# A two-layer graph network on one core: norms applied in halves, and layer 1's unit ends moved behind a copy

## The chip, the core and the metric

The kernel runs on one core of one Trainium2 chip. Its engines work side by side, each through its own list in order, and wait for one another by semaphores: TensorE (PE; its weight loads are PEld), VectorE (DVE), ScalarE (ACT), GpSimd (POOL), and SyncE (SP), which issues most of the transfers. The metric is device time of one launch in microseconds. The kernel before takes 3890.02 us, the median of 3 runs (3889.3 to 3892.25).

## The reference, cut to what matters

Eight graphs of 2048 nodes with 256 features share one adjacency matrix. Layer 0 is masked attention with a softmax inside each chunk of 256 keys, added over the chunks; layer 1 is graph attention. Each is followed by norms over the features:

```
# layer 0: four heads of 64, keys in chunks of 256
scores = clip(q . k / 8, -10, 10);  scores = where(mask == 0, -10, scores)
ctx = sum over chunks of softmax(scores within the chunk) @ v
out = layernorm(ctx @ Wo.T + bo + x) * gamma + beta
x   = layernorm(x + out)
# layer 1: four heads of 64
e = leaky_relu(s_src[j] + s_dst[i], 0.2), masked;  alpha = softmax(e)
x = layernorm(x + elu(alpha @ (x @ W)))
```

## The kernel before, in words

The order of the work is written out by hand (line 89). One program serves the eight graphs ("batches"). While batch b is in layer 0, batch b-1 is in layer 1 and batch b-2 in its closing norm, all interleaved.

Layer 0 of a batch is 64 *slots*. A slot is one chunk of 256 keys against 512 queries for two heads; 16 slots make a group of 512 queries, and the four groups are called q 0 to 3; i is the slot's place in the group. In slot s TensorE runs, in this order: scores of slot s+1 (`ps`, L360); the product of the first head (`pc`, L393); three tiles of layer 1 (`pa`, L709); the product of the second head (`pc` again). The two products share one PSUM buffer, since their pool has a single one (line 83), and ScalarE's copy to `raw` (L400) empties it each time. VectorE clips and masks the scores (`pr`, L371), inverts the sums (`rd`, L408), and makes layer 1's `e` (L689), one step of three tiles ahead of their use. ScalarE takes exponentials of `pr` (L383).

Layer 1 has 12 *units* of 16 tiles in a batch. At three tiles per slot a unit ends in slots i = 5, 10 and 15 of each group. Its end is a generator, `close` (L726), of four steps: `dn` (L732, 733) on VectorE; `hh` (L737), five or six activations on ScalarE; `ee` and `hp` (L741, 743) on ScalarE; `h` (L745) on VectorE. `rest(1)` runs one step. It is called at the head of `step` (L754), so between the two products of a slot: after the exponentials and ahead of the second head's copy.

`Between` carries the finished group of 512 queries from layer 0 to layer 1. Its steps are hung on slots by three tables: `AHEAD` at a slot's start, `BESIDE` after the scores (VectorE's share), `BEHIND` after the second copy. Two norms apply there: the first (`a.apply`, slot 7), then `scale` by gamma, `again` (the residual), statistics, the second (`finish`, slot 11). `Norm.apply` (L471) is four activations, one for each block of 128 nodes. `finish` also stores the result to DRAM (`x1D`, L533, from ScalarE's queue). `load` (slot 12) reads it back on SyncE's queue in squares of 32 (`x1t`, eight transfers, L262), `turn` (slot 14) transposes it on VectorE (`x1T`, L274), and `values` multiplies it by layer 1's weights (`pw`, L552) from slot 14 on. The last group of a batch goes another way, between the batches.

`Closing` does the same for the last norm: `add`, `stats` and `finish` (applied to `o`) in slots of q 0, as `CLOSING` says.

The tables of before:

```
AHEAD  = {12: load}
BESIDE = {..., 8: scale, 9: again + b2.stats((0, 1)), 10: b2.stats((2, 3)), 14: turn}
BEHIND = {..., 7: a.apply(y), 11: finish, 14: values((0,)), 15: values((1,))}
```

Of the kernel before, what the change touches and what calls it, by code (L numbers as in the profile page):

```python
# [8 lines left out]
F32 = mybir.dt.float32  # L9
# [8 lines left out]
P = 128  # L18
# [4 lines left out]
def adj_resnorm_kernel(  # L23
# [19 lines left out]
    nc = tc.nc  # L43
    B, N, F = x.shape
# [11 lines left out]
    QT = CH // P  # L56
# [23 lines left out]
    blocks = ctx.enter_context(tc.tile_pool(name="blocks", bufs=2))  # L80
# [28 lines left out]
    x1D = tc.dram_tile([B, N, F], F32, name="x1D")  # L109
# [75 lines left out]
    outgoing = []  # L185
# [61 lines left out]
    def by_node(dram, b, g):  # L247

        return dram[b, g * CH : (g + 1) * CH, :].rearrange("(t p) f -> p t f", p=P)
# [94 lines left out]
    def load_slab(s):  # L344
        q, hp, c = where[s]
        slab = slabs.tile([P, KT, CH], I8, tag="slab", name="slab")
        nc.sync.dma_start(out=slab, in_=clipD[q][:, KT * c : KT * (c + 1), :])
        slab_of[s] = slab
# [98 lines left out]
    class Norm:  # L447
# [20 lines left out]
                nc.gpsimd.tensor_tensor(self.rs, self.rs, nhalf, ALU.pow)  # L468
                nc.gpsimd.tensor_mul(self.off, self.off, self.rs)

        def apply(self, dst):  # L471
            for k in range(QT):
                nc.scalar.activation(  # L473
                    dst[:, k, :],
                    self.src[:, k, :],
                    AF.Identity,
                    bias=self.off[:, k : k + 1],
                    scale=self.rs[:, k : k + 1],
                )


    class Between:
# [45 lines left out]
            nc.vector.tensor_add(self.y, self.y, self.r)  # L528
            self.b2 = Norm(self.y, "b")

        def finish(self):
            self.b2.apply(self.y)
            nc.scalar.dma_start(out=by_node(x1D, self.b, self.g), in_=self.y)  # L533

        def load(self):
            self.t = load_turned(x1D, self.b, self.g, "x1t")
# [30 lines left out]

    AHEAD = {12: lambda o: o.load()}  # L570
    BESIDE = {
        1: [lambda o: o.bias()],
        4: [lambda o: o.add((0, 1))],
        5: [lambda o: o.add((2, 3)), lambda o: o.a.stats((0, 1))],
        6: [lambda o: o.a.stats((2, 3)), lambda o: o.shift()],
        8: [lambda o: o.scale()],
        9: [lambda o: o.again(), lambda o: o.b2.stats((0, 1))],
        10: [lambda o: o.b2.stats((2, 3))],
        14: [lambda o: o.turn()],
    }  # L580
    BEHIND = {
        3: lambda o: o.output((0, 1)),
        4: lambda o: o.output((2, 3)),
        7: lambda o: o.a.apply(o.y),
        11: lambda o: o.finish(),
        14: lambda o: o.values((0,)),
        15: lambda o: o.values((1,)),
    }
# [56 lines left out]
    class Layer1:  # L645
# [106 lines left out]
            )  # L752

        def step(self):  # L754
            self.rest(1)
            for _ in range(STEP):
                self.make()
                self.use()

    class Close:  # L760
# [9 lines left out]
            nc.vector.tensor_add(self.h, self.h, self.x)  # L770
            self.n = Norm(self.h, "c")

        def finish(self):
            o = blocks.tile([P, QT, F], F32, tag="y", name="o")
            self.n.apply(o)
            outgoing.append(lambda: nc.sync.dma_start(out=by_node(out, self.b, self.g), in_=o))

    class Closing:

# [4 lines left out]
        def do(self, s, beside=True, behind=True):  # L784
            for g, step in self.table.get(s, ()):
                if step == "load" and behind:
                    self.of[g] = Close(self.b, g)
                elif step == "finish" and behind:
                    self.of[g].finish()
                elif step == "add" and beside:  # L790
                    self.of[g].add()
                elif step == "stats" and beside:
                    self.of[g].n.stats((0, 1, 2, 3))
# [8 lines left out]
    for g in range(NCH):  # L802
# [11 lines left out]
        -1: [(0, "load")],  # L814
        0: [(0, "add"), (1, "load")],
        1: [(0, "stats")],
        2: [(0, "finish")],
        3: [(1, "add"), (2, "load")],
        4: [(1, "stats")],
        5: [(1, "finish")],  # L820
        7: [(2, "add"), (3, "load")],
        8: [(2, "stats")],
        10: [(2, "finish")],
        11: [(3, "add")],
        12: [(3, "stats")],
        13: [(3, "finish")],
    }
    CLOSING_ALONE = {
        -1: [(0, "load"), (1, "load")],
# [23 lines left out]
    lower = None  # L853
    for b in range(B):
        waug = blocks.tile([P, NT, H, D1], F32, tag="waug", name="waug")
        sd = small.tile([P, 2 * H, NT], F32, tag="sd", name="sd", bufs=1)
        if b == 0:
            for s in range(3):
                load_slab(s)
        scores(0)  # L860
        for u in range(KT):
            exps(0, u)
        if lower:
            for _ in range(STEP):
                lower.make()
        closing = Closing(b - 2, CLOSING) if b > 1 else None
        if closing:
            closing.do(-1)
        group = None
        for s in range(SLOTS):  # L870
            q, hp, c = where[s]
            i = s % QS
            send()
            if s + 3 < SLOTS:
                load_slab(s + 3)
            if i == 0:
                before = group
                group = Between(b, q - 1, sd, waug) if q else None
            if i == 1 and q:
                load_context(b, q - 1, 1)  # L880
            if i == QS // 2 + 1:
                load_context(b, q, 0)
            if group and i in AHEAD:
                AHEAD[i](group)
            if s == SLOTS - 1 and b + 1 < B:
                turns = [project(b + 1, g) for g in range(NCH)]
                turns[0].pop(0)()
            if s:
                normalize(s - 1)
            if s + 1 < SLOTS:  # L890
                scores(s + 1)

            if i == 3 and q:
                turn_context(q - 1, 1)
            if i == QS // 2 + 3:
                turn_context(q, 0)
            if group:
                for step in BESIDE.get(i, ()):
                    step(group)
            elif closing:  # L900
                closing.do(s, behind=False)
            product(s, 0)
            if s + 1 < SLOTS:
                for u in range(KT):
                    exps(s + 1, u)
            if lower:
                if b + 1 < B or s < SLOTS - LATE:
                    lower.step()
            elif masks.left():
                masks.step()  # L910
            product(s, 1)

            if before and i in AFTER:
                AFTER[i](before)
            if i == 0 and q:
                send_context(b, q - 1, 1)
            if i == QS // 2:
                send_context(b, q, 0)
            if group and i in BEHIND:
                BEHIND[i](group)  # L920
            elif closing and not q:
                closing.do(s, beside=False)
        normalize(SLOTS - 1)
        if lower and b + 1 < B:
            lower.rest(4)

        send()
        before = group
        gd, fs = factors(b, sd, waug)
        group = None  # L930
        every = tuple(range(QT))

        def begin():
            nonlocal group
            group = Between(b, NCH - 1, sd, waug)

        def ctx():
            context(NCH - 1, 1)

        steps = [  # L940
            lambda: group.bias(),
            lambda: group.output(every),
            lambda: group.add(every),
            lambda: (group.shift(), group.a.stats(every)),
            lambda: group.a.apply(group.y),
            lambda: (group.scale(), group.again(), group.b2.stats(every)),
            lambda: group.finish(),
            lambda: group.turn_all(),
            lambda: group.values((0, 1)),
            lambda: group.values((2, 3)),  # L950
        ]
        if b + 1 < B:
            (t0, k0, v0, q0), (l1, t1, k1, v1, q1), (l2, t2, k2, v2, q2), (l3, t3, k3, v3, q3) = turns
            order = [begin, t0, lambda: before.values((2, 3)), steps[0], k0, ctx, l1, v0, steps[1]]
            order += [t1, steps[2], q0, *steps[3:5], k1, l2, steps[5], v1, steps[6], t2, q1, l3]
            order += [steps[7], k2, steps[8], steps[9], v2, fs[0], t3, q2, fs[1], k3]
            order += [lambda: [load_slab(s) for s in range(3)], fs[2], v3, q3]
        else:

            step = lower.step  # L960
            order = [begin, lambda: before.values((2, 3)), steps[0], step, ctx, step, steps[1], step]
            order += [steps[2], step, steps[3], step, steps[4], step, steps[5], step, steps[6], step]
            order += [steps[7], step, steps[8], step, steps[9], step, fs[0], step, fs[1], step, fs[2]]
            order += [step, lambda: lower.rest(4)]
            assert sum(p is step for p in order) == LATE
        for piece in order:
            send()
            piece()
        send()
        lower = Layer1(b, gd, waug)  # L970
# [5 lines left out]
    for s in range(SLOTS + 1):  # L976
        send()
        if s < SLOTS:
            lower.step()
        else:  # L980
            lower.rest(4)
        closing.do(s)
        ending.do(s)
# [43 lines left out]
```

## Time and profile before

Time from the start of a slot's first `pc` matmul to the next slot's, batch 3, cut from the trace by hand (us). The other batches from 2 to 6 agree within 0.04 but for one slot; batch 1 has 6.03 in all of q 0, for it has no closing norm.

| i | 0 | 1 | 2 | 3 | 4 | 5 | 6 | 7 | 8 | 9 | 10 | 11 | 12 | 13 | 14 | 15 |
|---|---|---|---|---|---|---|---|---|---|---|---|---|---|---|---|---|
| q 0 | 6.03 | 6.04 | 6.60 | 6.03 | 6.03 | 6.71 | 6.03 | 6.03 | 6.03 | 6.07 | 6.03 | 6.03 | 7.13 | 6.58 | 6.03 | 6.03 |
| q 1 | 6.03 | 6.03 | 6.03 | 7.96 | 7.96 | 5.80 | 5.68 | 6.21 | 5.68 | 5.68 | 5.96 | 5.87 | 6.61 | 5.68 | 6.77 | 6.77 |
| q 2 | 6.77 | 6.77 | 5.68 | 7.61 | 7.61 | 5.68 | 5.68 | 6.12 | 5.68 | 5.68 | 5.89 | 5.87 | 6.60 | 5.68 | 6.77 | 6.77 |
| q 3 | 6.77 | 6.77 | 5.68 | 7.61 | 7.61 | 5.68 | 5.68 | 6.12 | 5.68 | 5.68 | 5.89 | 5.87 | 6.61 | 5.68 | 4.85 | |

How to read it: slots of equal content last equally long, so a longer one shows either more work for TensorE or a wait. Slots 3 and 4 hold the output projection, slots 14, 15, 0 and 1 the value projection of layer 1, up to q 1's slot 5 the units are six blocks wide, after it five. Slot 14 of q 3 has no scores behind it. Batch 0, without a layer below, has slots of 4.68 us, and so has batch 7 in the last 14 slots, whose steps of layer 1 are kept for later.

The 512 slots are about four fifths of the span of 3888.7 us; the rest are projections between the batches (67.6 us each after batches 2 to 6, from the last slot's start to the next batch's first), the start (84.0) and layer 1 of the last batch alone (267.9).

### The profile page before, as it was taken

To read this page: it belongs to the slowest core of one execution; us is meant where nothing else is said; L and a number is where in the kernel's file an instruction comes from. 1 tells how busy PE (TensorE), PEld (TensorE's weight loads), DVE (VectorE), ACT (ScalarE), POOL (GpSimd) and SP (SyncE) were. 2 spreads that over 40 slices of the span, in tenths; PEclk is the share of its full clock that TensorE was granted. 3 is DMA by queue.
4 is the path that set the end of the run, shared out by engine and by line. 5 is a ranking of instruction groups with operands and counts; after the bars stand their busy time and mean duration, and the time that the engine had idled before them with its cause. 6 is when DMAs were issued, how large, how long until landed. Compare 5 with 4: busy or idle time off the path is not lost. (4 is left out here: it accounts for less than half of the span.)

```text
span 3888.7 us, 160154 instructions
## 1 busy us (share of the span) xinstructions
PE 3696.5 (95%) x72068; PEld 2752.5 (71%) x72068; DVE 3204.7 (82%) x4810; ACT 1946.2 (50%) x3601; POOL 1384.4 (36%) x1202
## 2 busy tenths in 40 slices
PE   7988999999999999999999999999999999999787
PEld 4655577776777767776777767777677776776676
DVE  4776499985999779996999959998599977998798
ACT  3655445554555445554555545555455555555321
POOL 0444234342433333432433324434243333434310
PEclk9999999999999999999999999999999999999999
DMA  7642333333434343333433334333343334333354
GB/s 151 150 108 59 77 96 98 97 89 94 121 97 102 75 121 101 99 102 70 134 99 100 97 87 129 101 95 88 94 121 102 98 78 118 106 95 88 95 146 123
DMA packets 771328, 398.48 MB, mean 102 GB/s; under 512 B 442576, under 2 KB 735824, under 8 KB 770640
## 3 DMA queue, kind: packets, MB, share of 16 engines
q1 hardware_dynamic: 720640, 354.54, 35.9%
q10 hardware_dynamic: 50000, 33.70, 2.7%
q8 instruction: 563, 9.22, 1.0%
q14 instruction: 125, 1.02, 0.1%
HBM read 331.22 MB, written 56.89 MB: 100 GB/s over the span
## 5 line engine op out<-in xcount | busy, mean ns | idle before, releaser
L371 DVE SCALAR_TENSOR_TENSOR pr<-ps,slab 128x1024 f32<-128x1024 f32 x1024 | 1192.7, 1205 | 237.3 <-PE ps L360 234.0
L393 PEld LDWEIGHTS pc<-vaug,pr 128*64 128x64 f32 x32768 | 1041.6, 138 | 475.3 <-ACT raw L400 243.9
L689 DVE SCALAR_TENSOR_TENSOR e<-srow,gd,et 128x640 f32<-128x640 f32 (+1 forms) x1536 | 1348.0, 934 | 5.4 <-PE pa L709 5.4
L393 PE MATMUL pc<-vaug,pr 128*64 128x65 f32 x32768 | 1161.4, 224 | 68.9 <-ACT raw L400 63.1
L383 ACT ACTIVATE pr<-pr 128x1024 f32<-128x1024 f32 x1024 | 1052.1, 1057 | 249.3 <-DVE pr L371 234.5
L709 PE MATMUL pa<-waug,e 128*64 128x65 f32 x32768 | 1089.8, 224 | 41.0 <-DVE e L689 39.2
L709 PEld LDWEIGHTS pa<-waug,e 128*64 128x64 f32 x32768 | 1025.2, 139 | 70.3 <-DVE e L689 39.8
L360 PE MATMUL ps<-qT,kT 64*128 64x512 f32 x4096 | 1022.4, 617 | 9.1 <-DVE pr L371 7.0
L415 POOL TENSOR_TENSOR part<-raw,rd 128x512 f32<-128x512 f32 x448 | 467.9, 1044 | 1472.7 <-DVE rd L408 1460.1
L400 ACT COPY raw<-pc 128x260 f32<-128x260 f32 x1024 | 383.5, 375 | 1139.0 <-PE pc L393 1092.4
L417 POOL TENSOR_TENSOR acc<-acc,part 128x512 f32<-128x512 f32 x448 | 574.0, 1281 | 35.2
L360 PEld LDWEIGHTS ps<-qT,kT 64*128 64x128 f32 x4096 | 351.5, 186 | 332.1 <-issue 208.7
L408 DVE RECIPROCAL rd<-raw 128x8 f32<-128x8 f32 x512 | 101.5, 198 | 139.4 <-ACT raw L400 133.2
L415 POOL TENSOR_TENSOR acc<-raw,rd 128x512 f32<-128x512 f32 x64 | 66.8, 1043 | 366.1 <-DVE rd L408 365.3
L304 PE MATMUL pp<-xT,wk_sb 128*128 128x512 f32 x256 | 123.9, 628 | 47.0 <-DVE xT L274 32.3
L737 ACT ACTIVATE hh<-pa,dn 128x64 f32<-128x64 f32 x512 | 114.0, 319 | 101.3 <-DVE dn L733 101.3
L552 PE MATMUL pw<-w_sb,x1T 128*128 128x264 f32 x512 | 137.0, 403 | 2.6 <-DVE x1T L274 2.5
L468 POOL TENSOR_TENSOR rs_c<-rs_c,nhalf 128x4 f32<-128x4 f32 x32 | 55.6, 1738 | 227.5 <-DVE off_c L467 227.5
L508 PE MATMUL po<-wo_sb,qT 128*128 128x256 f32 x512 | 124.8, 389 | 0.0
L304 PEld LDWEIGHTS pp<-xT,wk_sb 128*128 128x128 f32 x256 | 48.3, 198 | 106.5 <-issue 49.6
L320 PE MATMUL pv<-wv_sb,xT 128*128 128x256 f32 x512 | 115.9, 379 | 0.0
L304 PE MATMUL pp<-xT,wq_sb 128*128 128x512 f32 x256 | 115.3, 593 | 0.0
(90 smaller groups left out, 1888.2 us busy)
## 6 DMA issues: line engine op xcount, KB each, us to landing
et<-edgeD SPq DMA_DIRECT2D x256, 320.0 KB, 3.2
slab<-clipD SPq DMA_DIRECT2D x512, 128.0 KB, 3.5
et<-edgeD SPq DMA_DIRECT2D x128, 384.0 KB, 3.5
srow<-rowD SPq DMA_DIRECT2D x64, 320.0 KB, 4.4
xp<-in_x_dram SPq DMA_DIRECT2D x256, 64.0 KB, 2.3
xg<-in_x_dram SPq DMA_DIRECT2D x32, 512.0 KB, 4.7
x1D<-y ACTq DMA_DIRECT2D x32, 512.0 KB, 3.1
x1g<-x1D SPq DMA_DIRECT2D x32, 512.0 KB, 5.9
```

Source lines behind the costliest of these rows:

```text
L304: nc.tensor.matmul(pp[:, c, :], lhsT=w[:, kc, c * P : (c + 1) * P], rhs=st["xT"][:, kc, :], start=(kc == 0), stop=(kc == KC - 1),)
L360: nc.tensor.matmul(ps[:, k, :], lhsT=kT[rows, hp, t * P : (t + 1) * P], rhs=qT[rows, hp, cols], start=True, stop=True,)
L371: nc.vector.scalar_tensor_tensor(pr, pss[u], -CLIP, slab[:, u, :].unsqueeze(1).to_broadcast([P, 2, CH]), op0=ALU.max, op1=ALU.min,)
L383: nc.scalar.activation(pr, pr, AF.Exp, scale=0.125)
L393: nc.tensor.matmul(pc[z * D : (z + 1) * D, i, :], lhsT=probs[s][u][:, k, i * P + z * D : i * P + (z + 1) * D], rhs=vaug[:, KT * c + u, 2 * ...
L400: nc.scalar.copy(raws[s][:, k], pc)
L415: nc.gpsimd.tensor_mul(part, raw[:, :, :, :D], rd.to_broadcast([P, 2, QT, D]))
L417: nc.gpsimd.tensor_add(accv, accv, part)
L508: nc.tensor.matmul(po[:, k, :], lhsT=qT[:, c, t * P : (t + 1) * P], rhs=wo_sb[:, c, :], start=(c == 0), stop=(c == KC - 1),)
L552: nc.tensor.matmul(pw[:, k, : F + 2 * H], lhsT=self.x1T[:, c, u * P : (u + 1) * P], rhs=w1_sb[:, c, :], start=(c == 0), stop=(c == KC - 1),)
L689: nc.vector.scalar_tensor_tensor(e[:, :w], self.rows[n][:, :w], self.gd[:, h, j : j + 1], self.edge[k // JG][:, j % JG, :w], op0=ALU.max, ...
L709: nc.tensor.matmul(self.pa[z * D : (z + 1) * D, i * D1 : (i + 1) * D1], lhsT=e[:, i * P + z * D : i * P + (z + 1) * D], rhs=self.waug[:, j ...
```

## The change

Each application of a norm is split into two blocks and two blocks, in neighbouring slots, so that no slot has all four on ScalarE. What depends on it moves along: `scale` from slot 8 to 9, the end of `finish` with its store from 11 to 12, `load` from 12 to 13; `turn` and `values` stay. And `rest(1)`, the step at a unit's end, goes from the head of `step` to behind the second product, so that ScalarE copies the second head's sums ahead of it. It is meant to keep ScalarE's long runs out of the way of the copies for which TensorE waits.

```diff
-        def apply(self, dst):
-            for k in range(QT):
+        def apply(self, dst, ks=range(QT)):
+            for k in ks:
...
-        def finish(self):
-            self.b2.apply(self.y)
-            nc.scalar.dma_start(out=by_node(x1D, self.b, self.g), in_=self.y)
+        def finish(self, ks=range(QT)):
+            self.b2.apply(self.y, ks)
+            if ks[-1] == QT - 1:
+                nc.scalar.dma_start(out=by_node(x1D, self.b, self.g), in_=self.y)
...
-    AHEAD = {12: lambda o: o.load()}
+    AHEAD = {13: lambda o: o.load()}
...
-        8: [lambda o: o.scale()],
-        9: [lambda o: o.again(), lambda o: o.b2.stats((0, 1))],
+        9: [lambda o: o.scale(), lambda o: o.again(), lambda o: o.b2.stats((0, 1))],
...
-        7: lambda o: o.a.apply(o.y),
-        11: lambda o: o.finish(),
+        7: lambda o: o.a.apply(o.y, (0, 1)),
+        8: lambda o: o.a.apply(o.y, (2, 3)),
+        11: lambda o: o.finish((0, 1)),
+        12: lambda o: o.finish((2, 3)),
...
         def step(self):
-            self.rest(1)
             for _ in range(STEP):
...
-        2: [(0, "finish")],
-        3: [(1, "add"), (2, "load")],
+        2: [(0, "half")],
+        3: [(0, "rest"), (1, "add"), (2, "load")],
         4: [(1, "stats")],
-        5: [(1, "finish")],
+        5: [(1, "half")],
+        6: [(1, "rest")],
...
-        10: [(2, "finish")],
+        9: [(2, "half")],
+        10: [(2, "rest")],
...
-        13: [(3, "finish")],
+        13: [(3, "half")],
+        14: [(3, "rest")],
...
             product(s, 1)
+            if lower:
+                lower.rest(1)
```

Outside the slots (between the batches and in the last batch's layer 1 alone) `rest(1)` is called ahead of `step` as before, and norms are applied whole.

More of the change, by code (lines that the diff above doesn't have):

```diff
@@ L771, in add, with finish @@
             self.n = Norm(self.h, "c")
[L773 to L776, printed above, removed]
+        def finish(self, ks=range(QT)):
+            if ks[0] == 0:
+                self.o = blocks.tile([P, QT, F], F32, tag="y", name="o")
+            self.n.apply(self.o, ks)
+            if ks[-1] == QT - 1:
+                outgoing.append(
+                    lambda: nc.sync.dma_start(out=by_node(out, self.b, self.g), in_=self.o)
+                )
     class Closing:
@@ L787, in do @@
                     self.of[g] = Close(self.b, g)
+                elif step == "half" and behind:
+                    self.of[g].finish((0, 1))
+                elif step == "rest" and behind:
+                    self.of[g].finish((2, 3))
                 elif step == "finish" and behind:
@@ L958, in adj_resnorm_kernel, with step @@
         else:
-            step = lower.step
+            def step():
+                lower.rest(1)
+                lower.step()
             order = [begin, lambda: before.values((2, 3)), steps[0], step, ctx, step, steps[1], step]
@@ L978, in adj_resnorm_kernel @@
         if s < SLOTS:
+            lower.rest(1)
             lower.step()
```

## The prediction

> **What bounds the kernel now.** I read four views in order: engine totals, wait list, the trace cut at the slots, and the timeline of one disputed stretch. The totals:
>
> ```profile
> PE 3696.5 (95%) x72068; PEld 2752.5 (71%) x72068; DVE 3204.7 (82%) x4810; ACT 1946.2 (50%) x3601; POOL 1384.4 (36%) x1202
> ```
>
> TensorE is nearly full and ScalarE half empty, so shortening ScalarE's work alone buys nothing; only a wait that reaches TensorE counts. The wait list (total us, times, longest) says which do:
>
> ```profile
> PEld pc L393 <- ACT raw L400: 243.9, 284, 3.1
> ...
> PE pc L393 <- ACT raw L400: 63.1, 104, 2.3
> ...
> PE pa L709 <- DVE e L689: 39.2, 33, 5.5
> ```
>
> The second line, 63.1 us, is the true idle time in which a product waits for the copy that empties its only PSUM buffer; the first includes waits of weight loads behind running matmuls. 63 us is the pool the change can draw on.
>
> Cutting the trace at the first `pc` matmul of each slot (table above) shows where: slots without a wait last 5.68 us (6.03 with six-bank units, 6.77 with a value projection). Over that floor lie, in q 1 to 3, slot 7 (+0.44 to +0.53), 10 (+0.21), 11 (+0.19) and 12 (+0.92); in q 0, slots 2 and 5 (+0.6, +0.7), 12 (+1.10) and 13 (+0.55). The timeline of q 2's slots 12 to 14 (start, duration):
>
> ```profile
> 1672.98 2.08 ACT L473 ACTIVATE y<-y,off_b,rs_b 128x256 f32<-128x256 f32 x4
> ...
> 1675.09 0.37 ACTq L533 DMA_DIRECT2D x1D<-y  x1
> ...
> 1676.21 2.19 ACT L383 ACTIVATE pr<-pr 128x1024 f32<-128x1024 f32 x2 [0.28 <-DVE pr L371]
> ...
> 1678.01 5.62 SPq L262 DMA_DIRECT2D x1t<-x1D  x8
> 1678.30 1.11 ACT L737 ACTIVATE hh<-pa,dn 128x64 f32<-128x64 f32 x5
> 1679.28 0.40 ACT L400 COPY raw<-pc 128x260 f32<-128x260 f32 x1
> 1679.73 1.15 PE L393 MATMUL pc<-vaug,pr 128*64 128x65 f32 x32 [0.68 <-ACT raw L400]
> ...
> 1683.24 0.45 ACT L741 ACTIVATE ee<-hh 128x320 f32<-128x320 f32 x1
> ...
> 1687.11 1.23 DVE L274 STREAM_TRANSPOSE x1T<-x1t 128x1024 f32<-128x1024 f32 x1
> ```
>
> See two things. `hh` stands before the copy, and `pc` waits for it: that is what the change removes. And `x1D` leaves at 1675.09, its re-read `x1t` begins only 2.92 us later, takes 5.62 us to issue, and `x1T` needs it at 1687.11: that is the chain the change moves.
>
> [...] SyncE waits for this store all 24 times:
>
> ```profile
> SPq L262 <- DMA x1D<-y: 199.7, 24, 12.0
> ```
>
> [...] VectorE idled for `x1t` in one of 24 turns. [...] `raw` (1679.28) starts only as `hh` (1678.30 + 1.11) ends.
>
> **The change, part by part.** No computation is added; instructions change places.
>
> *Unit's end behind the copy.* `dn` moves from slots 6, 11, 0 to the end of 5, 10, 15, `hh` to the end of 6, 11, 0, `ee`/`hp` to 7, 12, 1, `h` to 8, 13, 2. In q 1 to 3, slot 12: exps end at 1678.4, the copy is then done by 1678.7, so only the scores hold slot 13. `dn` and its reciprocal (0.12 and 0.19, start to start 0.26) now stand ahead of slot 11's `pr`, which shifts slot 12's start from 1673.13 to about 1673.3; from there `pc`, `pa`, `pc` and the scores reach slot 13 at 1679.17 instead of 1679.73. I take this 0.56 as the net saving, hence T14 (slot 14's start) 1684.85 in place of 1685.41.
>
> Slot 7: the same mechanism, but I cost it at nothing, since VectorE is full there:
>
> ```profile
> 1650.00:1679.00 29.00, 28.92 (x660) 22.16 (x660) 28.89 (x46) 18.40 (x33) 12.68 (x11) 1.00 0.35 91
> ```
>
> The columns are stretch, length, busy time of PE, PEld, DVE, ACT, POOL; VectorE works 28.89 of 29.00 us. TensorE starting slot 8 at 1649.5 in place of 1650.0 meets the same queue: in after's order `rd, pr, e, h, rd, pr, scale, again, stats, e, rd, pr`, with start-to-start steps 0.12, 2.22, 2.35, 0.39, 0.12, 2.22, 1.38, 1.24, 0.9, 2.35, 0.12 from 1650.03, slot 10's `pr` starts at 1663.4; before it did at 1663.55. Moving `scale` to slot 9 reorders this sum, it doesn't shorten it. Slots 10 and 11 keep or take over the excess.
>
> q 0, slots 12 and 13: `hh` (1.32) and `ee`/`hp` (0.92) leave the way of the copies. `pr` and `e` behind 2.6 us of statistics still arrive late, so of 1.10 + 0.55 I take 0.77, six times (batches 2 to 7): -4.6 us. Slots 2 and 5 wait for `e` behind the statistics (`pa` lasts 2.78 there, not 2.27), which stay: nothing.
>
> *Norms in halves.* An `apply` of four is 2.08 us of ScalarE, a half about 1.05. In the 5.68 us slot ScalarE needs 2.19 + 2 x 0.38, so both fit in its gap; first norm and closing norm gain nothing beyond the above. Without a lower layer (batch 0; batch 7, q 3) slot 12 runs 0.33 long because `apply` holds the next copy: four times -0.33.
>
> *The late half.* The second half of `finish` and with it the store go to the end of slot 12. Walk of q 2: exps to 1678.40, `raw` to 1678.66, `ee` and `hp` to 1679.3, two activations to 1680.4, then the store: 5.3 us later than 1675.09. From store to the last landing of `x1t` the trace gives 8.73 to 11.75 us, mean 10.34 over the 24 (store landing 2.9 to 5.0, then eight issues, the last landing 1.9 to 4.4 later). So landing is at 1690.7, the turn 0.3 later at 1691.05. That 0.3, and the rest of the chain, is measured in batch 0, where the load was late once:
>
> ```profile
> 408.63 1.25 DVE L274 STREAM_TRANSPOSE x1T<-x1t 128x1024 f32<-128x1024 f32 x1 [1.70 <-DMA xp<-in_x_dram]
> ...
> 409.93 1.16 PE L552 MATMUL pw<-w_sb,x1T 128*128 128x264 f32 x4 [1.83 <-DVE x1T L274]
> ```
>
> Turn to `pw` 1.3 us, VectorE idle 1.70, TensorE 1.83, slot 14 2.0 over its floor. In after, `turn` still stands in slot 14, so `pw` starts at 1692.35. Unstalled it would at T14 + 3.77 (measured in slot 14 of batch 3) = 1688.6. Stall: 3.7 us. Queued behind the turn on VectorE is `e` for slot 15's `pa`, due after T15 + 1, so it adds nothing; behind `pw` on TensorE the next scores and everything after. SyncE is held too, but slabs are loaded three slots ahead and edges 2.7, against some 5 us: nothing.
>
> Net per group in the full regime: +3.7 - 0.56 = +3.15; 20 groups, +63. Batch 0: slots of 4.68, store at T14 - 4.6, landing T14 + 5.74, turn + 6.04, `pw` + 7.33, against 2.77 unstalled (324.59 - 321.71, less the 0.11 by which that slot was long): +4.56, less 0.93 of mean stall it has already, less 0.33: +3.3, three times, +9.9. Batch 7, q 3: +4.56 - 0.19 - 0.33 = +4.0. With q 0's -4.6: **+72.3, 3962.3 us**. The projections between batches (67.6 us) and the tail (267.9) keep their order.
>
> **The rivals.** (1) *Hidden re-read, faster*: the load lands in time after all (8.7 us from store to landing, the shortest seen, is not enough; about 6.6 would be needed). Then 20 x -0.56 - 4.6 - 1.3 = -17: 3873; with slot 7's 0.5 kept too, 3863. For it: VectorE's lag might hide part of the stall, and ScalarE's copies are what the wait list names first. Against: 5.3 us later, while the slack of the case shown (landed about 1685.2, turned 1687.1) is 1.9. (2) *Short stall*: all re-reads take the shortest seen, 8.7 us: stall 2.1 instead of 3.7, 24 x 1.6 = 38 less: 3924. (3) *Longer stall*: the longest, 11.75, or SyncE's hold starves the edges: 24 x 1.4 = 34 more: 3996.
>
> **Numbers.** Forecast 0.76; short stall 0.1; longer 0.07; hidden 0.07. The range, 3926 to 3994, reaches to the second and third and takes in landing times about 1.5 us off the mean. Faster 0.06, same 0.02, slower 0.92.
>
> **What would show it.** In after: `x1T` idle before, some 4 us each for the DMA, and a wait of `pw` for `x1T` near 85 to 100 us in sum where before has 5.6; slot 14 near 10.5 us; slot 12 of q 1 to 3 at 5.7; slot 7 at 5.7 with slot 10 longer by as much; PE's wait of `pc` for `raw` well under 63. Slot 14 staying at 6.8 would prove me wrong.

## The result, and the profile after

The changed kernel takes 4026.68 us (median) against 3891.14 us for the kernel before: ratio 1.0351, 95% interval 1.0333 to 1.0369. The forecast was slower, 3962 us; the loss is 135.5 us where 72 were forecast, outside the range. The profiled executions differ by 131.6 us (spans 3888.7 and 4020.3), and that difference is accounted for below.

Engine totals of after:

```profile
PE 3755.3 (93%) x72068; PEld 2780.4 (69%) x72068; DVE 3209.9 (80%) x4810; ACT 1967.6 (49%) x3601; POOL 1398.3 (35%) x1202
```

The same instructions, yet TensorE is busy 58.8 us longer (3755.3 against 3696.5): work that is the same in number has become slower somewhere. Of the 58.8 us, 37.7 lie in slot 14 and 12.1 in slot 10. The wait list of after, the rows that answer to those of before and two new ones:

```profile
PEld pc L393 <- ACT raw L400: 188.7, 254, 4.1
...
PE pw L553 <- DVE x1T L274: 100.1, 24, 5.6
...
DVE x1T L274 <- DMA x1t<-x1D: 64.8, 16, 4.8
...
PE pa L711 <- DVE e L691: 38.3, 35, 5.9
...
PE pc L393 <- ACT raw L400: 35.2, 73, 3.3
```

The change did what it was meant to do: TensorE's wait for the copy fell from 63.1 to 35.2 us. In its place stands a wait of 100.1 us, once in each of the 24 groups that are turned inside the slots, for `x1T`. VectorE in turn waits for the re-read `x1t` in all 24: the row shown has 16 of them, and the view puts the other 8 (28.4 us) down to other transfers. In before TensorE's wait was this:

```profile
PE pw L552 <- DVE x1T L274: 2.5, 2, 1.8
```

Slot lengths, cut as before (batch 3, us; i 7 to 14):

| | 7 | 8 | 9 | 10 | 11 | 12 | 13 | 14 |
|---|---|---|---|---|---|---|---|---|
| q 2 before | 6.12 | 5.68 | 5.68 | 5.89 | 5.87 | 6.60 | 5.68 | 6.77 |
| q 2 after | 5.68 | 5.68 | 5.68 | 6.41 | 6.18 | 5.68 | 5.68 | 12.35 |

Timeline of q 2's slots 12 to 14 in after, the counterpart of the stretch shown of before:

```profile
1733.09 2.19 ACT L383 ACTIVATE pr<-pr 128x1024 f32<-128x1024 f32 x2 [0.58 <-DVE pr L371]
...
1735.18 0.36 ACT L400 COPY raw<-pc 128x260 f32<-128x260 f32 x1
1735.44 0.47 ACT L743 ACTIVATE ee<-hh 128x320 f32<-128x320 f32 x1
...
1736.17 1.09 ACT L473 ACTIVATE y<-y,off_b,rs_b 128x256 f32<-128x256 f32 x2
1737.29 0.37 ACTq L534 DMA_DIRECT2D x1D<-y  x1
...
1741.16 4.96 SPq L262 DMA_DIRECT2D x1t<-x1D  x8
...
1748.09 1.25 DVE L274 STREAM_TRANSPOSE x1T<-x1t 128x1024 f32<-128x1024 f32 x1 [3.62 <-DMA x1t<-x1D]
...
1749.39 2.13 PE L553 MATMUL pw<-w_sb,x1T 128*128 128x264 f32 x4 [3.91 <-DVE x1T L274]
1751.45 2.61 PE L360 MATMUL ps<-qT,kT 64*128 64x512 f32 x8
```

The copy now goes first, and `pc` no longer waits. But the store leaves 4.35 us ahead of slot 14's start (1741.64), where it left 10.3 us ahead; the turn starts 6.45 us into the slot instead of 1.7; TensorE idles 3.91 us. Then comes what the forecast did not have: the two `pw` matmuls (four records) take 2.13 us in place of 1.16, the scores 2.61 in place of 1.99. The same two in before:

```profile
1689.18 1.16 PE L552 MATMUL pw<-w_sb,x1T 128*128 128x264 f32 x4
1690.27 1.99 PE L360 MATMUL ps<-qT,kT 64*128 64x512 f32 x8
```

The windows view of this slot and of its end after the wait (columns as in the prediction; the last three are PEclk, the granted clock, the busy share of the DMA engines, and GB/s):

```profile
1741.64:1753.99 12.35, 8.44 (x138) 5.91 (x136) 7.29 (x11) 3.17 (x6) 4.30 (x4) 0.86 0.55 113
...
1749.40:1753.99 4.59, 4.59 (x12) 2.20 (x12) 3.14 (x5) 0.45 (x2) 1.96 (x2) 0.63 0.30 77
```

The same slot in before:

```profile
1685.41:1692.18 6.77, 6.77 (x138) 5.06 (x136) 6.54 (x9) 3.10 (x6) 2.85 (x3) 1.00 0.66 188
```

In before the clock of slot 14 is 1.00. In after it is 0.63 in the 4.6 us behind the wait. The trace's clock record has 23 stretches at half clock that begin in a slot 14, of 3.41 or 6.83 us each, 109.2 us in sum; in before none begins there.

### The profile page after: what moved, and what is told of

It reads as the page before. It is cut to its first block, busy times and chain, and to the rows that moved or that the text cites. A ratio compares the mean times of both kernels' runs of the same rounds, so it can differ in the third digit from the quotient of the medians.

```text
span 4020.3 us, 160132 instructions
## 1 busy us (share of the span) xinstructions
PE 3755.3 (93%) x72068; PEld 2780.4 (69%) x72068; DVE 3209.9 (80%) x4810; ACT 1967.6 (49%) x3601; POOL 1398.3 (35%) x1202
## 5 line engine op out<-in xcount | busy, mean ns | idle before, releaser
L393 PE MATMUL pc<-vaug,pr 128*64 128x65 f32 x32768 | 1169.7, 225 | 40.5 <-ACT raw L400 35.2
L711 PE MATMUL pa<-waug,e 128*64 128x65 f32 x32768 | 1102.1, 224 | 41.3 <-DVE e L691 38.3
L360 PE MATMUL ps<-qT,kT 64*128 64x512 f32 x4096 | 1046.0, 629 | 11.3 <-DVE pr L371 6.9
L417 POOL TENSOR_TENSOR acc<-acc,part 128x512 f32<-128x512 f32 x448 | 574.4, 1282 | 35.2
L553 PE MATMUL pw<-w_sb,x1T 128*128 128x264 f32 x512 | 154.9, 442 | 100.1 <-DVE x1T L274 100.1
L553 PEld LDWEIGHTS pw<-w_sb,x1T 128*128 128x128 f32 x512 | 98.7, 206 | 124.1 <-DVE x1T L274 103.4
L560 ACT COPY waug<-pw 128x256 f32<-128x256 f32 (+1 forms) x104 | 44.3, 426 | 164.2 <-PE pw L553 164.2
```

The costliest lines, as they stand in the source:

```text
L360: nc.tensor.matmul(ps[:, k, :], lhsT=kT[rows, hp, t * P : (t + 1) * P], rhs=qT[rows, hp, cols], start=True, stop=True,)
L393: nc.tensor.matmul(pc[z * D : (z + 1) * D, i, :], lhsT=probs[s][u][:, k, i * P + z * D : i * P + (z + 1) * D], rhs=vaug[:, KT * c + u, 2 * ...
L417: nc.gpsimd.tensor_add(accv, accv, part)
L553: nc.tensor.matmul(pw[:, k, : F + 2 * H], lhsT=self.x1T[:, c, u * P : (u + 1) * P], rhs=w1_sb[:, c, :], start=(c == 0), stop=(c == KC - 1),)
L711: nc.tensor.matmul(self.pa[z * D : (z + 1) * D, i * D1 : (i + 1) * D1], lhsT=e[:, i * P + z * D : i * P + (z + 1) * D], rhs=self.waug[:, j ...
```

## The experiments

**Theory**: the late half of the second norm delays the store, the re-read lands after the turn is due, TensorE waits about 4 us in each of 24 groups, and behind the wait it runs at half clock for a while (0.63 in the 4.6 us above). **Rivals**: the part of slot 14 that the wait does not explain comes from SyncE's queue, which the re-read holds up (late slabs and edges); the re-read is emitted too late, whatever the store does; or the moved unit ends, or the halves, cost by themselves.

In the sums below "slot 14" is the total over the 24 groups: 146.0 us in before, of which 2.5 is TensorE's wait for `x1T`, so 143.5 without it; 281.2 in after.

### The late half alone (`late_half`)

```diff
 # kernel before; apply and finish take the blocks as in the change
-    AHEAD = {12: lambda o: o.load()}
+    AHEAD = {13: lambda o: o.load()}
...
-        11: lambda o: o.finish(),
+        11: lambda o: o.finish((0, 1)),
+        12: lambda o: o.finish((2, 3)),
```

> The kernel before with only the second application split over slots 11 and 12 and the re-read emitted in slot 13; unit ends, first norm and closing norm as before. Theory 'late store': nearly all of the loss is here: slot 14 of 12 to 14 us in q 1 and 2, TensorE waiting about 100 us for the turned tile, 4020 to 4045. Rival 'unit ends cost': well under half of the loss, below 3950.

Measured: 4024.21 us, ratio 1.0341 (1.0327 to 1.0355). Wait list:

```profile
PE pw L553 <- DVE x1T L274: 92.3, 24, 5.4
```

This one split, with the store and the re-read that move with it and nothing else of the change, gives the whole loss. Slot 14 grows by 129.8 us and the other slots not at all (slots 7 to 13 of q 1 to 3 keep the lengths of before within 0.03 us in 158 of 168 cases). So the moved unit ends are not needed for the loss.

### The re-read without its wait for the store (`load_x`)

```diff
 # changed kernel
-            self.t = load_turned(x1D, self.b, self.g, "x1t")
+            self.t = load_turned(x, self.b, self.g, "x1t")
```

> The changed kernel, but the re-read of slot 13 fetches the same rows of the input x instead of the stored norm (its values are then wrong for layer 1): the transfers are the same, only the wait for the store is gone. Theory 'late store': no stall in slot 14 (6.8 us), 3870 to 3885 in all, the other slots as in the changed kernel. Rival 'late load' (emission at slot 13 is itself too late, whatever the store does): slot 14 still 2 us or more over its floor, over 3920.

Measured: 3896.94 us, ratio 1.0020 (1.0013 to 1.0027), above the expected 3870 to 3885. The wait for `x1T` fell to this:

```profile
PE pw L553 <- DVE x1T L274: 11.7, 21, 3.0
```

The same eight transfers, emitted in the same slot, are nearly in time when they need not wait for the store: for the group shown (q 2, batch 3) SyncE starts them 5.45 us ahead of slot 14, where after starts them 0.48 ahead. It is the store that is late. The expectation of no stall at all was not met, and the miss in the total is slot 14's: it is 12.2 us over before, 9.0 of them in four groups, and at most 0.44 in any other. The other slots are as in the changed kernel (slots 7 to 13 of q 1 to 3: -11.7 us in both).

### TensorE kept busy during the wait (`warm` and `warm8`)

```diff
 # changed kernel, in values
                 pw = psM.tile([P, 1, CH], F32, tag="psM", name="pw")
+                if us[0] == 0:
+                    for _ in range(14):  # 8 in warm8
+                        nc.tensor.matmul(
+                            pw[:, 0, :F],
+                            lhsT=wo_sb[:, 0, :P],
+                            rhs=wo_sb[:, 1, :],
+                            start=True,
+                            stop=True,
+                        )
```

> The changed kernel with 14 extra matmuls of 256 columns (about 3.5 us of TensorE work, by the 0.25 us of one output-projection matmul) put ahead of slot 14's value projection, into the same PSUM tile, which the projection then overwrites. They need nothing from the re-read and fill TensorE's wait for it. Theory 'clock': of slot 14's mean excess of some 6 us about 4 is the wait, the rest is TensorE at half clock [...]; with TensorE kept busy the half-clock stretches in slot 14 vanish, the slot lasts about 10.7 us where it lasted 12.8, and the kernel some 50 us less: 3965 to 3985. Rival 'queue': the rest comes from SyncE's held queue (late slabs, edges); then slot 14 stays near 12.8 and the time near 4025, or more.

Measured with 14: 4028.79 us, 1.0355 (1.0341 to 1.0369). My size was wrong: one such matmul took 0.43 us, not 0.25 (the record shows two halves for each, and I had taken one half for the whole). Fourteen last 6.04 us, longer than the wait, and slot 14 lasts 12.81 us in nearly every group of q 1 and 2, which is 6.77 + 6.04. Length and total are those that the rival 'queue' named, but the fill itself makes them, so this run doesn't decide between the two; it does show slot 14 without a single half-clock stretch (mean granted clock of the run 0.989, of after 0.978).

> As warm, with 8 extra matmuls in place of 14. One took 0.43 to 0.45 us there (28 records for 14 matmuls, 6.04 us of added slot time at steady clock), so 8 are about 3.5 us and end before the turned tile is there, some 4.1 us into the wait. Theory 'clock': TensorE's idle spell shrinks to under 1 us, the clock stays full, and slot 14 lasts its floor of 6.77 plus the wait of about 4.1: 10.5 to 11.2 in q 1 and 2, where the changed kernel had 12 to 14; total 3970 to 3990, though TensorE does more work. Rival 'queue': slot 14 stays at 12 to 14, total 4020 or more.

Measured with 8: 3986.34 us, 1.0251 (1.0235 to 1.0267), some 40 us below the changed kernel though TensorE does 192 matmuls more. Timeline of the same group (q 2, batch 3), the fill and what follows, then the window of the whole slot:

```profile
1726.06 3.72 PE L551 MATMUL pw<-wo_sb 128*128 128x256 f32 x16
...
1730.74 1.16 PE L562 MATMUL pw<-w_sb,x1T 128*128 128x264 f32 x4 [0.96 <-DVE x1T L274]
1731.83 1.99 PE L360 MATMUL ps<-qT,kT 64*128 64x512 f32 x8
```

```profile
1722.30:1733.75 11.45, 10.49 (x154) 8.02 (x153) 7.14 (x11) 3.17 (x6) 2.78 (x3) 1.00 0.47 96
```

`pw` and the scores are back at 1.16 and 1.99 us, the clock at 1.00. The books: fill 24 x 8 x 0.43 = 82.6 us plus the remaining wait of 18.0 makes 100.6, as much as the wait of 100.1 in after. What slot 14 has beyond 143.5 and this is 281.2 - 143.5 - 100.1 = 37.6 us in after, and 249.7 - 143.5 - 100.6 = 5.6 us here. A second cut of the traces, which needs no figure for the fill, is sharper: from the first `pw` matmul to the end of slot 14, the 24 groups take 56.8 us in before, 93.1 in after and 56.4 with 8. So the work behind the wait is 36.3 us slower in after and not slower at all here, and the 5.6 us lie ahead of `pw`. The tile comes no sooner and the re-read holds SyncE's queue as before, so the rival 'queue' is out: the extra time is the clock's. In `late_half` the first sum leaves 40.0.

### The turn one slot later (`turn15`)

```diff
 # changed kernel
-        14: [lambda o: o.turn()],
+        15: [lambda o: o.turn()],
...
-        14: lambda o: o.values((0,)),
-        15: lambda o: o.values((1,)),
+        15: lambda o: o.values((0,)),
...
-    AFTER = {0: lambda o: o.values((2,)), 1: lambda o: o.values((3,))}
+    AFTER = {
+        0: lambda o: o.values((1,)),
+        1: lambda o: o.values((2,)),
+        2: lambda o: o.values((3,)),
+    }
```

> The changed kernel with the turn in slot 15 instead of 14, and the four value products in slots 15, 0, 1, 2 instead of 14, 15, 0, 1 (in the last group of the slots the second one moves behind the slots). Nothing else. Theory 'late store': the tile lands about 6.3 us after slot 14's start, so a turn some 7.5 us after it waits for nothing; slots 14 to 2 at their floors, no half clock; total as load_x without its stray waits: 3880 to 3897. Rival 'the halves and unit ends cost by themselves': above 3905.

Measured: 3883.19 us, 0.9980 (0.9973 to 0.9987). With everything of the change in place and only the readers of the re-read moved (the turn and the value products), the loss is gone and a gain of 0.2% stays. TensorE's wait for `x1T` nearly goes:

```profile
PE pw L553 <- DVE x1T L274: 3.9, 3, 2.5
```

### The second norm whole again (`whole_finish`), and the unit ends alone (`unit_end`)

```diff
 # changed kernel (whole_finish)
-    AHEAD = {13: lambda o: o.load()}
+    AHEAD = {12: lambda o: o.load()}
...
-        11: lambda o: o.finish((0, 1)),
-        12: lambda o: o.finish((2, 3)),
+        11: lambda o: o.finish(),
```

> The changed kernel with the second norm whole in slot 11 again and the re-read in slot 12; unit ends behind the copy, first norm and closing norm in halves as in the change. Theory: slot 14 back at 6.77 and no half clock there; slot 7 at its floor of 5.68; slots 10 and 11 at 6.4 and 6.2 as in the changed kernel; slot 12 at about 6.3, since hh and four activations (1.1 + 2.1 us) now stand behind one another ahead of the next copy. Sum over slots 7 to 13 within 0.3 us of before; 3880 to 3893. Rival 'unit ends cost': above 3900.

Measured: 3907.32 us, 1.0045 (1.0031 to 1.0059). Slots 7, 10, 11 and 14 as expected; slot 12 was 6.85, not 6.3, and the time lies where the rival 'unit ends cost' had it. The next run tests that rival alone.

```diff
 # kernel before (unit_end)
         def step(self):
-            self.rest(1)
             for _ in range(STEP):
...
             product(s, 1)
+            if lower:
+                lower.rest(1)
```

> The kernel before with only the unit ends moved behind the second product; norms whole, in their old slots. Theory: slot 7 at or near its floor; slots 10 and 11 longer by 0.3 to 0.5 each, since dn and h now stand ahead of the next pr on the full VectorE; slot 12 about 6.85 as in whole_finish, since hh and four activations stand in a row ahead of the next copy; in q 0 slot 9 about 0.6 longer and slots 12 and 13 shorter. Sum about +10: 3893 to 3910, as whole_finish. Rival 'halves cost': this one is at or below before (3890), and whole_finish's loss is the halves'.

Measured: 3903.52 us, 1.0036 (1.0023 to 1.0049). So the unit ends behind the copy, without halves, are a small loss of their own, and the halves of the first and the closing norm cost next to nothing (whole_finish is 16.7 us over before in the profiled executions, unit_end 14.5). The timeline of q 2 (batch 3), where slot 12 lasts from 1675.10 to 1681.96:

```profile
1674.69 0.36 ACT L400 COPY raw<-pc 128x260 f32<-128x260 f32 x1
1674.94 1.14 ACT L737 ACTIVATE hh<-pa,dn 128x64 f32<-128x64 f32 x5
...
1675.94 2.10 ACT L473 ACTIVATE y<-y,off_b,rs_b 128x256 f32<-128x256 f32 x4
1678.07 0.37 ACTq L533 DMA_DIRECT2D x1D<-y  x1
1678.53 0.38 ACT L400 COPY raw<-pc 128x260 f32<-128x260 f32 x1 [0.49 <-ACT y L473]
...
1678.96 1.15 PE L393 MATMUL pc<-vaug,pr 128*64 128x65 f32 x32 [0.96 <-ACT raw L400]
```

`hh` left the way of one copy and stands, together with a whole norm, in the way of the next: with the store's issue the two hold `raw` until 1678.53, and `pc` waits 0.96. That is what the halves are for: in after, with half a norm behind `hh`, slot 12 is at its floor. In sums over all batches (us against before, profiled executions):

| slots | after | whole_finish | unit_end | act_behind |
|---|---|---|---|---|
| q 1 to 3, 7 | -9.3 | -7.8 | -9.4 | -7.8 |
| q 1 to 3, 10 and 11 | +17.9 | +16.3 | +15.1 | +7.8 |
| q 1 to 3, 12 | -20.5 | +4.7 | +5.1 | -15.2 |
| q 0, 9 | +4.0 | +3.4 | +4.0 | 0.0 |
| q 0, 12 and 13 | -8.1 | -7.8 | -7.0 | -4.5 |

### Only ScalarE's steps behind the copy (`act_behind`)

The rows of slots 10 and 11 and of q 0's slot 9 have a loss in every version with VectorE's steps moved. This version of the kernel before leaves `dn` and `h` at the head of the step and moves `hh` and `ee`/`hp` alone behind the copy, one slot later where a norm is applied (`rest_of` runs the next step of a unit's end only if it is of the kind asked for):

```diff
 # kernel before; due: 1 when ScalarE's step is next, 2 when VectorE's
         def step(self):
-            self.rest(1)
+            self.moved = False
+            self.rest_of(2)
...
             product(s, 1)
+            if lower and i not in (7, 11, 13):
+                lower.rest_of(1)
```

> The kernel before with only ScalarE's steps of a unit's end (hh; ee and hp) moved behind the second copy, and put off by one slot where a norm is applied there (slots 7, 11, 13); VectorE's steps (dn, h) stay at the head of the step, norms and re-read as before. Theory: slot 12 of q 1 to 3 at its floor (0.92 saved, 20 times), q 0's slots 12 and 13 shorter by 0.8 to 1.5 in sum (6 times), slot 7's 0.5 lost again in slots 10 and 11 where VectorE is full; 3860 to 3875, faster than both. Rival 'VectorE binds everywhere': slot 12's gain is lost elsewhere too, 3885 to 3892.

Measured: 3870.86 us, 0.9950 (0.9938 to 0.9963): faster than both kernels, if by half a per cent only; the interval leaves out 1, as do those of the three runs before. Wait list:

```profile
PE pc L393 <- ACT raw L400: 30.5, 49, 2.1
```

TensorE's wait for the copy is halved (63.1 before), norms stay whole, and the re-read keeps its place. Slot 12 falls to 5.85 us, not quite to its floor of 5.68. A third of slot 7's and 12's gain (7.8 of 23.0 us) is given back in slots 10 and 11 even here. Whether it is VectorE's fullness alone that takes it, no run separates.

## Why the prediction was wrong

The direction and the start of the loss, the late store, were forecast, and the chain up to TensorE's wait held step by step. The size failed, by one missing term above all. The sum of the forecast against the profiled executions (us):

| term | forecast | measured |
|---|---|---|
| TensorE's wait for `x1T` | +89.2 | +97.6 |
| half clock after the wait | not in the sum | +37.6 |
| q 1 to 3, slots 7 to 13 | -12.5 | -11.7 |
| q 0 | -4.6 | -0.9 |
| start, between batches, tail | 0 | +8.9 |
| sum | +72 | +132 |

- *The late half.* Store forecast 4.45 us ahead of slot 14 (1680.4 against 1684.85), measured 4.35. Turn forecast 6.2 us into the slot, measured 6.45 in the group shown, 5.3 to 7.6 over all. The landing times of before carried over, as forecast: from store to last landing 10.34 us on average in before, 10.64 in after. (SyncE waits for ScalarE's store 24 times in after, 193.4 us in sum.) The wait as a whole came out 9% above the forecast (97.6 against 89.2).
- *The stall.* Forecast "3.7 us" for a group, and then "slot 14 near 10.5 us". **This is the step that failed.** It took the stall as the whole price, with TensorE resuming at full speed: the forecast's slot 14 held 6.77 us of work whatever went before it. It held for one group only: batch 6, q 2, after a wait of 3.42 us with no half-clock stretch behind it, lasted 10.26. The others lasted 12 to 14.4 us in q 1 and 2. All 22 waits of 3.5 us and more (up to 5.57) drew a half-clock stretch of 3.41 or 6.83 us, and so did one of 2.78 us, while the one of 3.42 us drew none: the length of the wait alone doesn't settle it, and no run tests what does. The forecast had no such cost. `warm8` shows the term by taking it away.
- *Slot 7 costs nothing.* Right: slot 7 fell to its floor (-9.3), and slots 10 and 11 took more than that back (+17.9). The forecast gave the reason, VectorE at 28.89 of 29.00 us, and said that slot 10 would be longer by as much as slot 7 is shorter: in the group shown slot 7 lost 0.44 and slot 10 gained 0.52. Slot 11 gained 0.31 more, so slot 12 starts 0.39 us later than in before, counted from slot 7's start, where the walk had 0.17.
- *Slot 12.* Forecast at 5.7 us (the walk itself gives 5.87); it is 5.68, its floor, and 20.5 us are saved there. So slots 7 to 13 of the group shown come out 0.53 us shorter in sum, where 0.56 was forecast: the sum is right, though it is made of larger gains and losses than the walk had.
- *q 0.* 8.1 us saved in slots 12 and 13, but `h` at the end of slot 8 stands ahead of the next `pr`, which slot 9 pays with 4.0 us, as `unit_end` shows too; slot 8 has one stray pause of TensorE of 2.25 us in batch 3, with a half-clock stretch behind it. The forecast had costed `h`'s move at nothing there.
- *SyncE held.* Costed at nothing; the fill experiment bears it out, for with the fill slot 14 from `pw` on is no longer than in before (56.4 us against 56.8 over the 24 groups).
- *Between the batches.* Forecast unchanged; +6.5 us there, +3.0 in `late_half`. What makes these is open.
- *The sign in the wait list.* The 5.6 us given for before are two rows, 2.5 of TensorE and 3.1 of its weight loads; the 100.1 of after compare with the 2.5.

The rival of the longer stall came nearest (3996, still 31 us short), but not for its reasons: landings were not that late (10.64 us on average, 11.72 at most, where it had 11.75), and SyncE's queue was not the cause. The range was cut at landing times and left out that waiting itself could have a price.

## What to carry to other kernels

The read-back through DRAM is a chain that got no shorter here when it started later (10.34 us on average in before, 10.64 in after): before moving the first link of such a chain by a slot, count the slack at its last one, here 1.9 us against a shift of 6.0 (the store left 10.3 us ahead of slot 14, now 4.35). Don't price a new wait of TensorE at its length alone: behind 23 of the 24 here the clock was at half for 3.41 or 6.83 us, which came to 1.6 us on top of a mean wait of 4.2, and one wait of 2.78 us was enough to draw it. And when ScalarE's work is moved out of the way of one copy, look at the next copy and at VectorE's steps that move along: only the pieces that were in the way should move.

## What the runs showed of the hardware

TensorE's clock fell to half at 23 of the 24 waits of after, for 3.41 us (14 times) or 6.83 us (9 times), though the core's other engines and its transfers went on (from 1745.50 to 1749.40, in the wait shown above, VectorE was busy for 1.31 us, ScalarE for 0.40, the DMA engines for 85%); 37.6 us of slot time were lost to it (36.3 by the cut at `pw`), 1.6 us on each. Filling the wait with matmuls whose results are thrown away saved 1% of the changed kernel's time.

The length of the wait alone doesn't settle whether the clock falls. Two groups of batch 6, each with its wait and the work behind it (q 2, where `pw` starts at 3181.25, then q 3, where it starts at 3284.44):

```profile
3177.83:3181.25 3.42, 0.00 (x2) 0.01 (x1) 1.30 (x2) 0.42 (x2) 0.00 (x0) 1.00 0.70 185
3181.25:3184.25 3.00, 3.00 (x12) 1.36 (x12) 3.00 (x5) 0.45 (x2) 0.44 (x1) 1.00 0.03 11
3281.66:3284.44 2.78, 0.01 (x2) 0.00 (x0) 1.30 (x2) 0.43 (x2) 0.00 (x0) 1.00 0.58 92
3284.44:3289.81 5.37, 5.37 (x97) 4.83 (x99) 2.42 (x4) 0.82 (x3) 2.33 (x2) 0.68 0.69 158
```

In q 2 the clock stays at 1.00 behind a wait of 3.42 us; `pw` and the scores last 1.16 and 1.99 us, as in before, which is the same test as `warm8` within one run. In q 3, behind a wait of only 2.78 us, half clock begins at 3285.34 and lasts 3.41 us. What makes the difference no run tests.

The nine long stretches begin 0.6 to 3.2 us before `pw`, while TensorE still idles, the fourteen short ones from 0.25 us before its start to 0.94 us after it.

By the clock record an upper estimate of the loss is 109.2 / 2 = 54.6 us. Of the 109.2 us about 12 lie ahead of `pw`; that takes some 6 us off. For the remaining 11 us no run names the cause.
